# The attention product of a GAT layer as seven matmuls instead of eight, with one buffer fewer and new orders

## The chip, the cores and the metric

The kernel runs on one core of a Trainium2 chip. A core has five engines that work side by side, each through its own queue in order: TensorE (PE, matmuls, with a separate queue PEld for loading weights), VectorE (DVE), ScalarE (ACT), GpSimd (POOL) and SyncE (SP), which here only starts DMAs. Matmul results go to PSUM, 8 banks of 2 KB in each of 128 partitions[...]. The metric is the time of one execution on the device in microseconds. The profile is one further execution, recorded by the hardware profiler.

## What is computed

64 graphs of 256 nodes with 512 features, a 256x256 adjacency for each, all in float32. Two layers, each x = x + layer(relu(layernorm(x)), adjacency).

```python
# layer 0: gated attention, 8 heads of 64
q, k, v = (h @ W.T for W in (Wq, Wk, Wv))
c = softmax(where(adj != 0, q k^T / 8, -inf)) @ v          # per head
gate = sigmoid(concat(c, h) @ Wg.T + bg)
out0 = gate * h + (1 - gate) * c
# layer 1: GAT, one head
Wh = h @ W
e = leaky_relu(Wh a1 [:, None] + Wh a2 [None, :], 0.2)
out1 = elu(softmax(where(adj == 0, -1e9, e)) @ Wh)
```

## The kernel before

A graph's 256 nodes are two tiles of 128 (t = 0, 1), its 512 features two halves of 256 (n = 0, 1). The kernel is written as some 150 named steps for each graph. A table, PLAN, gives each step a time relative to the graph's own start; graph g is shifted by g x ROUND (48), and all steps of all graphs are sorted by that number. This sorted list is the order in which each engine gets its instructions; nothing is reordered later. So about four graphs are in work at once, and after the first few a round repeats for each graph. MOVED holds tables of their own for the first three and the last three graphs, ONCE the order of loading and preparing the weights.

**Products in Strassen's form.** q and k together (qk), v, z (the gate) and wh (Wh) are each a product of a 2x2 block matrix with another. `product` (matmuls on line 369) makes seven block products, named 1 to 7, in three PSUM banks: a takes 1 and then 2, b takes 6, 7 and 4, c takes 5 and 3. Between them partial sums are read out: u1 = a after 1 (copied by ScalarE, line 386), then on VectorE (line 382) u2 = b after 6 + u1, u3 = b after 7 + u1, and the outputs c11 = c after 5 + u3, c10 = b after 4 + u1, c01 = c after 3 + u2; c00 is a after 2, copied by ScalarE. Product 7 adds into the bank that u2 has to have read, 4 into the one that u3 has read, 3 into the one that c11 has read. The sums of the left operand (four for each, steps Sh, Sg, Sc, S1) are GpSimd's (line 353), those of the weights are made once on VectorE (line 308).

**Layer 0.** Step nm0 (ScalarE, line 437) makes the normed tokens h, th turns 32x32 blocks on VectorE (line 445), sh writes them to DRAM in four DMAs (there_h, line 453), fh fetches them transposed (hT, line 460). qk, scores (sc.0 and sc.1, line 566, eight matmuls into four banks each), max on VectorE (line 576), exp on ScalarE (line 586), scale on GpSimd (602) or ScalarE (600), turn, send and fetch to transpose (there_e, eT), we (line 626, banks pc), cT (ScalarE copy, 635), tc (VectorE, into cb), sent and fetched as c. z and the gate: tanh, diff (d<-d,c on GpSimd, 674), plus (x<-x,c on GpSimd, 679), mix (688) and res (x<-d,x, 692) on VectorE. again (ScalarE) makes h once more for the gate.

**Layer 1.** Statistics st1 on VectorE, root1 on GpSimd (rs_l, 427), nb1 on VectorE, nm1 on ScalarE into h1, th1, sh1, fh1 as in layer 0 (there_h and h1T in the profile), wh, ej, lo, lk, gm, gx (the softmax's exponentials), then tg, sg, fg to transpose (there_g, egT). Step po (line 803) multiplies the attention by wh in plain form: for each t four matmuls of 128x128 by 128x256 into one bank, eight for each graph. neg (VectorE, 817: min(po x rec, 0)) and pos (ScalarE, 823: relu(po x rec)) read the bank, xn (827) takes exp of neg, elu (834) and add (GpSimd, 842) finish, and x is stored. For the last two graphs (and the first two in layer 0) transposes go through TensorE instead of DRAM.

**Buffers.** SBUF tiles come from pools by tag: "h" has two buffers and serves h, cb and h1 in turn; "tmp" has five, "e" five, "x" five. A step that writes into a tile waits until the tile that had the buffer before is read for the last time, its DMAs included. In PSUM a tile takes one of eight banks, fixed when the program is built.

The order on TensorE in a steady round before the change: qk.1, z.4 and z.3 of an earlier graph, qk.6, v.1, qk.2, v.6, qk.7, v.5, qk.5, qk.4, po of t=0, qk.3, v.7, v.2, po of t=1, sc.0, we, sc.1, v.3, v.4, and then wh, ej and z of earlier graphs mixed.

Of the kernel before, what the change touches and what calls it, by code (L numbers as in the profile page):

```python
# [23 lines left out]
load@-50.672 st0.0@-48.955 st0.1@-47.821 root0@-38.184 nb0@-37.123 nm0.1@-29.56 nm0.0@-28.012 th.1@-27.761  # L24
th.0@-24.55 edges@-18.194 sh@-17.486 fh@-8.895 qk.1@-5.698 Sh.0@-2.801 Sh.1@-2.517 qk.6@0.316 v.1@0.417
Sh.2@0.475 qk.u1@0.958 qk.2@1.809 v.6@2.371 mask@3.53 qk.u2@3.72 qk.7@4.221 v.5@5.516 qk.5@6.175 qk.u3@7.606
Sh.3@7.626 qk.4@8.199 qk.c11@8.333 qk.c10@9.2 v.u1@9.714 v.u2@9.914 again.1@10.022 qk.3@10.809 qk.c01@10.827
v.7@10.9 v.2@10.953 qk.c00@12.201 sc.0@14.892 max.011@16.85 max.010@18.632 v.u3@21.472 exp.010@22.747
max.000@23.034 v.c11@23.409 max.001@24.188 sc.1@24.213 exp.000@24.365 exp.011@24.661 v.3@24.788 max.110@24.806
max.101@24.817 exp.001@24.929 v.4@26.032 max.100@26.733 rec.00@26.942 exp.101@27.067 v.c01@27.226 exp.110@27.532  # L30
v.c10@27.587 exp.100@29.503 rec.01@31.748 rec.10@32.989 scale.000@33.015 scale.001@34.279 max.111@34.283
turn.000@34.863 exp.111@35.153 scale.011@35.273 turn.001@35.815 scale.101@37.555 rec.11@37.814 turn.101@40.403
v.c00@41.809 scale.010@41.838 scale.100@42.033 send.00@43.292 turn.100@43.322 scale.111@43.998 scale.110@44.728
turn.111@45.825 turn.010@46.602 turn.011@46.632 turn.110@47.102 send.01@49.833 send.10@50.742 Sg.0@50.828
fetch.00@56.979 send.11@57.3 Sg.1@61.926 Sg.3@62.766 fetch.01@63.435 fetch.10@65.008 again.0@66.751 we.01@67.384
fetch.11@67.637 we.00@68.492 we.10@69.53 we.11@70.025 cT.0@70.71 Sg.2@71.512 cT.1@71.604 Sc.0@75.485 z.1@77.916
tc.0@78.544 tc.1@79.25 Sc.1@79.36 z.6@81.96 Sc.2@82.915 z.u1@84.089 z.u2@84.109 sc_c@85.464 z.2@86.278 fc@87.664
z.7@88.275 z.5@89.361 z.u2b@90.783 z.u3@91.761 z.4@92.198 diff.1@93.249 Sc.3@93.522 diff.0@93.841 z.c11@94.163
z.c10@95.683 z.c10b@95.767 z.3@95.773 z.c11b@96.156 plus.1@96.892 tanh.11@98.557 z.c00@98.842 z.c01@99.798
plus.0@99.907 tanh.10@100.162 tanh.00@100.302 mix.1@100.406 res.1@101.571 tanh.01@101.661 mix.0@102.238  # L40
st1.1@102.485 res.0@102.53 st1.0@102.632 root1@102.977 nb1@103.936 nm1.1@103.944 th1.1@103.981 nm1.0@104.039
th1.0@104.288 sh1@113.156 fh1@115.687 S1.0@120.46 S1.1@120.733 wh.1@122.864 wh.6@123.284 wh.u1@123.492
wh.u2@124.276 S1.2@126.087 S1.3@127.493 wh.7@128.378 wh.5@129.278 wh.u3@129.668 wh.c11@129.965 wh.3@130.015
wh.4@130.67 wh.c01@131.832 wh.2@132.003 ej@132.825 wh.c10@133.653 wh.c00@134.025 lo.0@134.129 lo.1@134.703
lk@135.599 gm@135.616 gx.1@140.75 gx.0@141.02 tg@141.763 sg@143.83 gr@152.036 fg@153.077 po.0@153.781
pos.0@153.792 neg.0@153.922 xn.0@156.41 elu.0@157.474 po.1@158.645 add.0@158.767 pos.1@159.243 neg.1@160.27
xn.1@162.323 elu.1@166.01 add.1@166.438 store.1@174.205 store.0@174.205
# [3 lines left out]
load@-167.262 st0.0@-166.518 st0.1@-149.893 nb0@-119.1 nm0.0@-93.712 again.1@-91.245 nm0.1@-79.836  # L51
again.0@-64.37 th.1@-44.14 Sh.0@-41.696 Sh.1@-39.058 Sh.2@-33.746 qk.1@-32.762 edges@-32.058 qk.6@-24.624
qk.u1@-22.066 qk.2@-21.372 qk.u2@-20.805 Sg.0@-17.521 qk.7@-12.436 v.1@-9.392 Sh.3@-8.979 v.6@-8.391
qk.c00@-6.667 qk.u3@-5.057 qk.4@-4.888 Sg.1@-0.322 mask@0.698 qk.5@1.593 qk.c10@3.209 sc.0@5.644 v.u1@9.942
qk.c11@9.945 max.001@10.33 max.011@10.718 Sg.2@13.35 max.000@14.194 qk.3@14.931 exp.001@15.477 qk.c01@15.562
v.u2@15.703 exp.000@15.706 max.010@16.308 sc.1@17.042 max.100@17.52 rec.00@18.128 v.7@18.379 max.101@19.595
exp.100@20.258 max.110@21.168 v.2@21.336 v.u3@21.429 v.5@22.311 scale.001@23.416 max.111@23.712 exp.101@23.777
scale.000@23.974 exp.110@24.415 rec.10@24.965 exp.111@25.826 turn.001@26.665 turn.000@28.936 v.4@29.176
exp.011@29.336 v.c11@29.596 v.c00@30.188 v.3@32.053 rec.11@32.575 scale.101@34.163 v.c10@34.571 exp.010@34.694
turn.101@34.778 rec.01@35.256 scale.110@36.123 scale.100@36.302 scale.011@37.337 turn.100@37.479 send.00@38.912  # L60
send.10@39.674 v.c01@40.035 scale.111@42.42 scale.010@43.268 turn.111@43.418 turn.110@44.351 fetch.00@45.699
turn.010@48.526 Sg.3@48.553 turn.011@48.931 send.11@49.968 send.01@50.543 fetch.10@54.389 fetch.11@60.135
we.00@61.1 we.10@64.692 fetch.01@65.017 we.11@65.565 we.01@66.842 cT.1@67.419 cT.0@68.77 Sc.0@70.118 tc.0@70.581
z.1@70.838 tc.1@73.212 Sc.1@73.23 z.u1@73.542 Sc.2@73.866 z.6@75.497 z.u2@77.891 Sc.3@78.433 z.2@80.627
z.7@81.61 z.5@82.138 z.u2b@83.128 z.u3@85.566 z.4@85.721 z.c11@87.076 z.c00@88.495 sc_c@90.404 tanh.00@91.263
z.3@91.318 z.c10@91.713 fc@93.294 diff.1@94.619 z.c10b@95.258 z.c11b@97.525 tanh.10@98.184 plus.1@98.373
tanh.11@99.383 diff.0@99.752 plus.0@99.825 mix.1@100.146 res.1@101.338 z.c01@102.596 tanh.01@103.055
st1.1@103.531 mix.0@104.285 res.0@104.338 st1.0@104.726 root1@106.188 nb1@107.795 nm1.0@110.078 nm1.1@110.383
th1.0@110.556 th1.1@110.644 sh1@111.628 fh1@113.083 S1.0@119.104 S1.1@120.807 wh.1@121.954 wh.u1@122.591
wh.6@123.635 S1.2@123.913 wh.u2@125.129 S1.3@125.627 wh.5@125.743 wh.7@125.989 wh.2@126.27 wh.u3@126.753  # L70
wh.c11@126.985 wh.4@127.999 wh.3@130.011 wh.c01@131.159 ej@132.88 wh.c10@134.879 lo.1@135.625 wh.c00@135.71
lo.0@137.207 lk@137.282 gm@138.475 gx.1@139.758 gx.0@140.997 gr@141.831 tg@142.453 sg@146.007 fg@149.698
po.1@155.192 po.0@155.734 pos.1@156.08 neg.1@156.318 neg.0@156.913 pos.0@159.131 xn.1@162.457 xn.0@163.013
elu.1@163.216 elu.0@164.233 add.1@164.844 add.0@166.667 store.1@177.808
""",
    1: """
load@-79.223 st0.0@-50.22 st0.1@-47.29 root0@-42.386 nb0@-38.757 edges@-37.434 nm0.0@-33.357 nm0.1@-32.922
th.1@-31.457 qk.1@-22.884 Sh.0@-20.22 Sh.1@-17.198 qk.u1@-17.092 Sh.2@-15.14 qk.6@-15.121 v.1@-13.274 qk.2@-8.08
qk.u2@-4.892 qk.7@-4.473 qk.c00@-3.706 qk.5@-1.564 v.5@0.189 qk.u3@1.902 Sh.3@2.194 v.6@2.96 qk.4@4.184
qk.c11@6.483 v.u1@7.021 qk.c10@7.937 v.u2@8.66 mask@8.958 qk.3@9.075 v.7@10.93 qk.c01@10.959 v.u3@11.262  # L80
sc.0@12.739 max.010@13.434 max.011@16.175 exp.010@16.871 max.001@20.08 max.000@20.575 sc.1@20.654 max.100@21.042
v.4@21.539 v.c11@21.681 max.111@21.684 exp.001@22.615 exp.000@23.152 exp.011@23.363 rec.00@23.965 v.3@23.997
max.101@24.041 exp.111@24.627 max.110@25.446 scale.000@26.187 v.c01@26.675 exp.100@27.482 exp.101@27.764
v.2@28.539 turn.000@29.046 rec.10@29.721 scale.001@31.771 exp.110@32.274 v.c00@32.326 rec.11@33.207
turn.001@33.213 scale.110@33.397 scale.100@33.543 v.c10@35.49 turn.100@36.991 scale.111@37.616 rec.01@37.977
scale.101@38.036 turn.101@39.099 scale.010@39.388 scale.011@39.76 turn.110@40.735 turn.111@44.635
turn.011@47.032 turn.010@47.774 send.00@48.222 send.10@51.087 send.01@52.398 Sg.2@55.238 send.11@56.725
fetch.00@57.149 fetch.10@57.246 fetch.01@58.584 fetch.11@60.705 Sg.0@61.477 we.01@63.116 we.00@64.106
we.10@65.881 Sg.1@66.592 cT.0@66.999 we.11@67.458 cT.1@68.314 Sc.0@68.508 z.1@69.658 tc.1@69.999 again.0@70.426
Sc.1@70.475 tc.0@71.17 z.6@71.96 Sc.2@77.177 sc_c@78.231 Sg.3@79.357 z.u1@79.468 z.2@84.425 z.u2@85.881  # L90
z.7@86.159 z.5@87.606 z.u2b@88.997 z.u3@90.833 Sc.3@92.191 z.c00@93.028 z.4@93.628 z.c11@93.691 fc@95.203
diff.0@95.45 z.c10@96.011 z.c11b@96.41 tanh.00@96.646 z.c10b@96.785 again.1@97.345 tanh.10@97.415 z.3@97.662
plus.1@99.074 tanh.11@99.574 z.c01@100.685 diff.1@100.815 tanh.01@101.285 mix.0@102.146 mix.1@102.203
plus.0@102.369 res.1@103.318 res.0@103.554 st1.1@103.742 st1.0@103.854 root1@104.013 nb1@105.63 nm1.0@106.015
# [819 lines left out]
```

## Time and profile before

| | us |
|---|---|
| median of 3 runs | 3134.52 (3133.42 to 3135.0) |
| the profiled execution, its own time | 3136.5 |
| its span, first to last instruction | 3134.6 |
| TensorE busy in the span | 3104.0 |
| VectorE, GpSimd, ScalarE busy | 2465.1, 1818.2, 1458.2 |
| one steady round (from one graph's qk to the next one's) | 48.07 |

The span is the time on the core; 1.9 us lie around it. Busy times of engines overlap, so their shares don't add up. A group in the profile's list names line, engine, operation and tiles, then count, busy time, mean length in ns, and the idle time ahead of it with what ended it. A matmul in float32 appears as two records. In the views by time a row merges like instructions that follow each other, with start and length.

### The profile page before, as it was taken

Reading aid. Unit: us, or ns where it says so; the run is one execution under the profiler, and the core shown is the slowest. Engines: PE = TensorE matmul, PEld = TensorE weight load, DVE = VectorE, ACT = ScalarE, POOL = GpSimd, SP = SyncE. Lnnn points to the kernel's source line nnn. Section 1 sums busy time; section 2 is a strip of 40 time slices with the busy share of each in tenths; the row PEclk is TensorE's granted clock in tenths of the full one; section 3 lists DMA queues with packets and bytes.
Section 4 is the critical chain, followed back from the end, with each engine's and each line's share of the span. In section 5 each row is a group of like instructions: output and inputs, shape, how many; then the busy total and the mean of one; then the engine's idle time right before and its main releaser. Section 6 shows DMA issues by size and latency. Waiting matters only on the chain.

```text
span 3134.6 us, 61537 instructions
## 1 busy us (share of the span) xinstructions
PE 3104.0 (99%) x19668; PEld 2708.9 (86%) x19668; DVE 2465.1 (79%) x6310; ACT 1458.2 (47%) x4039; POOL 1818.2 (58%) x2502
## 2 busy tenths in 40 slices
PE   9999999999999999999999999999999999999997
PEld 8887888888888888888888888888888888888885
DVE  8887787877877878778778778787787787877875
ACT  4444454454454454544544545445445444454452
POOL 4555565565655655656556556566565565565654
PEclk9999999999999999999999999999999999999998
DMA  7776777777777777777777777777777777777763
GB/s 222 188 196 171 194 197 184 198 188 193 199 188 191 195 186 195 194 189 201 189 185 201 183 196 197 183 200 189 191 201 184 194 198 185 196 189 193 195 160 94
DMA packets 1107154, 593.18 MB, mean 189 GB/s; under 512 B 687632, under 2 KB 1032720, under 8 KB 1106832
## 3 DMA queue, kind: packets, MB, share of 16 engines
q1 hardware_dynamic: 1106832, 589.25, 72.3%
q8 instruction: 158, 2.59, 0.4%
q14 instruction: 164, 1.34, 0.1%
HBM read 306.45 MB, written 282.59 MB: 188 GB/s over the span
## 4 chain that ended last, share of the span: by engine, by line
PE 96%; DVE 2%; DMA 1%; issue 0%; ACT 0%; SPq 0%; POOL 0%; DVEq 0%; ACTq 0%
PE pmb_qk L369 11%; PE pmb_z L369 10%; PE ps L566 8%; PE pc L626 7%; PE pmc_qk L369 7%; PE po L803 7%; PE pma_z L369 7%; PE pma_qk L369 7%; PE pmc_z L369 7%; PE pmb_wh L369 5%; PE pmb_v L369 5%; PE pmc_v L369 4%; PE pmc_wh L369 3%; PE pma_wh L369 3%; PE pma_v L369 3%
## 5 line engine op out<-in xcount | busy, mean ns | idle before, releaser
L586 ACT ACTIVATE e<-e,low 128x256 f32<-128x256 f32 x1024 | 507.9, 501 | 177.8 <-DVE low L576 177.8
L842 POOL TENSOR_TENSOR x<-x,pos 128x512 f32<-128x512 f32 x126 | 160.9, 1278 | 619.0 <-DVE pos L834 619.0
L576 DVE CUSTOM_DVE_ANT_0 e<-ps,mask 128x256 f32<-128x256 f32 x1024 | 375.9, 418 | 40.3 <-PE ps L566 39.2
L437 ACT ACTIVATE h<-x,nb_l,rs_l 128x512 f32<-128x512 f32 x256 | 200.0, 805 | 410.4 <-DMA eT<-there_e 215.0
L602 POOL TENSOR_SCALAR e<-e,rec 128x256 f32<-128x256 f32 x768 | 354.7, 482 | 24.9 <-DVE rec L593 20.7
L608 DVE STREAM_TRANSPOSE eb<-e 128x512 f32<-128x512 f32 x512 | 336.1, 684 | 6.4 <-DMA there_e<-eb 5.7
L566 PE MATMUL ps<-qk 64*128 64x256 f32 x2048 | 257.7, 390 | 0.5 <-ACT neg L827 0.5
L803 PE MATMUL po<-wh,egT 128*128 128x256 f32 x1024 | 245.8, 383 | 4.3 <-DMA egT<-there_g 2.5
L566 PEld LDWEIGHTS ps<-qk 64*128 64x128 f32 x2048 | 192.0, 186 | 60.0 <-DVE low L576 22.9
L817 DVE TENSOR_SCALAR neg<-po,rec 128x512 f32<-128x512 f32 x128 | 95.9, 750 | 183.4 <-ACT pos L823 168.5
L684 ACT ACTIVATE z<-z 128x256 f32<-128x256 f32 x256 | 93.5, 409 | 309.5 <-POOL z L391 190.3
L626 PE MATMUL pc<-eT,v 128*64 128x256 f32 x2048 | 235.6, 382 | 0.0
L427 POOL TENSOR_TENSOR rs_l<-ve_l,mhalf 128x2 f32<-128x2 f32 (+1 forms) x129 | 89.8, 696 | 248.4 <-DVE ve_l L423 232.3
L803 PEld LDWEIGHTS po<-wh,egT 128*128 128x128 f32 x1024 | 192.0, 193 | 30.2 <-DMA egT<-there_g 2.9
L445 DVE STREAM_TRANSPOSE h<-h 128x512 f32<-128x512 f32 x248 | 174.8, 707 | 52.2 <-DMA eT<-there_e 32.6
L626 PEld LDWEIGHTS pc<-eT,v 128*64 128x64 f32 x2048 | 141.1, 137 | 86.3 <-DVE neg L817 18.6
L674 POOL TENSOR_TENSOR d<-d,c 128x512 f32<-128x512 f32 x128 | 164.0, 1282 | 80.1 <-DMA c<-there_c 80.0
L679 POOL TENSOR_TENSOR x<-x,c 128x512 f32<-128x512 f32 x128 | 200.3, 1565 | 0.0
L586 ACT ACTIVATION_READ_ACCUMULATOR e<-e,low 128x1 f32 x1024 | 195.7, 191 | 0.0
L391 POOL TENSOR_TENSOR z<-z,bias 128x256 f32<-128x256 f32 x128 | 90.6, 727 | 168.3 <-DVE z L382 168.2
L416 DVE BATCH_NORM_STATS2 bs_l<-x 128x6 f32<-128x512 f32 x256 | 173.5, 678 | 8.0 <-DMA x<-in_x_dram 5.8
L823 ACT ACTIVATE pos<-po,rec 128x512 f32<-128x512 f32 x128 | 87.9, 687 | 187.2 <-PE po L803 173.9
(152 smaller groups left out, 8141.4 us busy)
## 6 DMA issues: line engine op xcount, KB each, us to landing
there_e<-eb SPq DMA_DIRECT2D x256, 512.0 KB, 3.9
eT<-there_e SPq DMA_DIRECT2D x1024, 128.0 KB, 3.6
there_h<-h SPq DMA_DIRECT2D x496, 128.0 KB, 3.5
there_c<-cb SPq DMA_DIRECT2D x64, 512.0 KB, 2.9
c<-there_c SPq DMA_DIRECT2D x256, 128.0 KB, 3.4
x<-in_x_dram SPq DMA_DIRECT2D x63, 512.0 KB, 5.0
out_dram<-x SPq DMA_DIRECT2D x63, 512.0 KB, 3.1
hT<-there_h SPq DMA_DIRECT2D x248, 128.0 KB, 3.2
```

What stands on the lines that cost most here:

```text
L369: nc.tensor.matmul(s[name, key][(slice(None), *cols)], lhsT, rhs, start=first and i == 0, stop=last and i == len(mms) - 1, skip_group_chec ...
L416: nc.vector.bn_stats(bs, s["x"][:, t, :])
L437: nc.scalar.activation(out, s["x"][:, t, :], AF.Relu, bias=s["nb", layer][:, t:t + 1], scale=s["rs", layer][:, t:t + 1])
L445: nc.vector.transpose(h, h)
L566: nc.tensor.matmul(s["ps", half, jj, i][:, t, :], qk[r:r + DK, 0, jj, t * P:(t + 1) * P], qk[r:r + DK, 1, jj, :], start=True, stop=True,)
L576: nc.vector.tensor_tensor_reduce(e[:, i, t, :], s["ps", half, jj, i][:, t, :], s["mask"][:, t, :], -SCALE, HUGE, ALU.add, ALU.min, accum_o ...
L586: nc.scalar.activation(e, e, AF.Exp, bias=s["low", half][:, jj, i, t:t + 1], scale=-1.0, accum_out=sums[:, jj, i, t:t + 1])
L602: nc.gpsimd.tensor_scalar(e, e, rec, 1.0, ALU.mult, ALU.mult)
L608: nc.vector.transpose(eb[:, :, 4 * i:4 * i + 4, :].rearrange("p b n c -> p n b c"), e)
L626: nc.tensor.matmul(pc[i * DK:(i + 1) * DK, jj, :].rearrange("p (t a c) -> p t a c", t=NT, c=32), s["v"][:, kc, hd * DK:(hd + 1) * DK], s[" ...
L679: nc.gpsimd.tensor_tensor(xt, xt, s["c"][t], ALU.add)
L803: nc.tensor.matmul(po[:, n, :], s["egT"][:, t, kc, :], to_wh(s, g, kc, n)[:, :HH], start=(kc, n) == (0, 0), stop=(kc, n) == (NT - 1, 1), s ...
```

## The change

Step po becomes a `product` too, for all graphs but the last. Its left operand is the transposed attention egT (four 128x128 blocks), its right one the four 128x256 blocks of wh. Each block product is a single matmul (two records). The sums of both operands are GpSimd's, made anew for each graph: Sp.0 to Sp.3 (128x128, into a tile of "tmp") and Rp.0 to Rp.3 (128x256, three in a tile R of a new pool, the fourth in place in wh). The totals u1, u2, u3, c00 to c11 are those of every product; the outputs go to SBUF tiles po of "tmp". neg and pos then read po there, and pos writes in place, so that its own tile is gone. The last graph keeps the old form, as step at.

The pool "h" has one buffer instead of two. h, cb and h1 of the graphs in work now follow each other in that one buffer, each after the sends of the one before have landed.

All tables (PLAN, MOVED, ONCE) are new, so every engine's order changes. The order on TensorE in a steady round is now: qk.1, qk.6, z.3, qk.7, qk.2, qk.5, qk.4, v.6, v.2 (of the graph before), qk.3, po.1, po.6, v.1, po.7, po.5, v.5, po.2, po.4, po.3, sc.0, v.7, we, sc.1, wh.1, v.3, v.4, wh.6, z.1, wh.7, wh.5, z.6, wh.3, wh.2, wh.4, ej, z.5, z.7, z.2, z.4. On VectorE the part that follows u2 of qk is: mix.1, z.c01, res.1, statistics of t=1, mix.0, u3 of qk, res.0, statistics of t=0, c11 of qk, half a turn.100, nb1, c10 of qk, the other half, th1.1, th1.0, a reciprocal, u2 of po, c01 of qk, mask, u3, c11 and c10 of po, nb0, u2 of v, c01 of po, neg.0, max. On ScalarE: tanh, nm1.1, nm1.0, u1 of po, c00 of qk, c00 of v, u1 of v, c00 of po, nm0.1, nm0.0 (of the graph three later), two exp, pos.0, two exp, xn.0, cT.0, again.0, cT.1. On GpSimd: two z biases, scale, diff.1, plus.1, diff.0, plus.0, Sh.3, scale, root1, Sg.0, Rp.1, Sp.0, Sp.1, Sp.2, root0, Sg.1, Sp.3, Rp.3. On SP: there_h of h1 (four), eT (four), h1T (four), there_h of h (four).

The diff, without the tables:

```diff
-        "x": 5, "mask": 3, "hT": 3, "S": 3, "qk": 2, "v": 1, "wh": 1, "e": 5,
-        "cT": 1, "z": 2, "h": 2, "tmp": 5, "U": 3,
+        "x": 5, "mask": 3, "hT": 3, "S": 3, "qk": 2, "v": 1, "wh": 1, "R": 1, "e": 5,
+        "cT": 1, "z": 2, "h": 1, "tmp": 5, "U": 3,
...
+    def left_sum(o, k):
+        return (
+            (o[5], o[8], o[4], ALU.add), (o[6], o[5], o[1], ALU.subtract),
+            (o[7], o[1], o[8], ALU.subtract), (o[3], o[2], o[6], ALU.subtract),
+        )[k]
+
+    def right_sum(o, k):
+        return (
+            (o[7], o[3], o[5], ALU.subtract), (o[6], o[7], o[1], ALU.add),
+            (o[5], o[5], o[1], ALU.subtract), (o[4], o[2], o[6], ALU.subtract),
+        )[k]
...
-    def product(name, shape, todo, dst, biased=False):
+    def product(name, shape, todo, dst, biased=False, until=B):
...
         def multiply(g, n):
+            if g >= until:
+                return
...
-    @step("po.0", "po.1")
+    def left_po(s, g):
+        p, S = s["egT"], lazily(s, "Sp", lambda: new("tmp", [P, 4, P], f"Sp_{g}"))
+        a11, a21, a12, a22 = p[:, 0, 0, :], p[:, 1, 0, :], p[:, 0, 1, :], p[:, 1, 1, :]
+        return {1: a11, 2: a12, 3: S[:, 3, :], 4: a22, 5: S[:, 0, :], 6: S[:, 1, :], 7: S[:, 2, :], 8: a21}
+
+    @step(*each("Sp", 4))
+    def attention_sums(s, g, k):
+        if g < B - 1:
+            nc.gpsimd.tensor_tensor(*left_sum(left_po(s, g), k))
+
+    def right_po(s, g):
+        t = lazily(s, "Rp", lambda: new("R", [P, 3, HH], f"Rp_{g}"))
+        b11, b12, b21, b22 = (s["wh"][:, k, n, :HH] for k in range(NT) for n in range(2))
+        return {1: b11, 2: b21, 3: b22, 4: t[:, 2, :], 5: b12, 6: t[:, 0, :], 7: t[:, 1, :]}
+
+    @step(*each("Rp", 4))
+    def value_sums(s, g, k):
+        if g < B - 1:
+            nc.gpsimd.tensor_tensor(*right_sum(right_po(s, g), k))
+
+    def to_po(s, g, t, n):
+        return lazily(s, ("po", t), lambda: new("tmp", [P, 2, HH], f"po_{g}_{t}"))[:, n, :]
+
+    product("po", [P, HH], lambda s, g, n: [((), left_po(s, g)[n], right_po(s, g)[n])], to_po, until=B - 1)
+
+    @step("at.0", "at.1")
     def attend(s, g, t):
+        if g < B - 1:
+            return
...
     def pos(s, g, t):
-        s["pos", t] = elu_part("pos", g, t)
         po = s["po", t].rearrange("p n f -> p (n f)")
+        s["pos", t] = po if g < B - 1 else elu_part("pos", g, t)
         nc.scalar.activation(s["pos", t], po, AF.Relu, scale=s["rec1"][:, t:t + 1])
```

## The prediction

> **What bounds the kernel now.** I read the page first (busy shares and the chain that ended last), then the busy time in stretches, then the waits of TensorE, then one round of 48.07 us in order of time.
>
> ```profile
> PE 3104.0 (99%) x19668; PEld 2708.9 (86%) x19668; DVE 2465.1 (79%) x6310; ACT 1458.2 (47%) x4039; POOL 1818.2 (58%) x2502
> ...
> PE 96%; DVE 2%; DMA 1%; issue 0%; ACT 0%; SPq 0%; POOL 0%; DVEq 0%; ACTq 0%
> ...
> L803 PE MATMUL po<-wh,egT 128*128 128x256 f32 x1024 | 245.8, 383 | 4.3 <-DMA egT<-there_g 2.5
> ```
>
> The columns of the next view are length, then busy time of PE, PEld, DVE, ACT and POOL with their instruction counts.
>
> ```profile
> 800.00:1200.00 400.00, 400.00 (x2563) 351.44 (x2562) 318.05 (x809) 184.84 (x511) 235.34 (x323) 1.00 0.75 194
> 3050.00:3100.00 50.00, 45.14 (x215) 36.69 (x215) 29.83 (x62) 17.45 (x42) 31.73 (x39) 0.93 0.49 141
> 3100.00:3120.00 20.00, 13.03 (x53) 9.62 (x52) 12.02 (x23) 5.42 (x10) 7.09 (x8) 0.91 0.07 27
> ```
>
> TensorE is busy for all 400 us of the middle stretch, with full clock; of its 30.6 idle us 3.3 lie in the first 60, 6.1 between 260 and 300, where the pipeline fills, and 19.6 after 3060. No other engine comes near: of 48.07 us a round, DVE works 38.2, POOL 28.3, ACT 22.2. So in some 61 steady rounds each matmul taken out is worth its own time, if nothing new makes PE wait.
>
> One round in order of time (start, length, engine, line, operation):
>
> ```profile
> 1536.38 1.90 PE L803 MATMUL po<-wh,egT 128*128 128x256 f32 x8
> 1538.12 1.05 PE L369 MATMUL pmc_qk<-Sh,wq_sb 128*128 128x128 f32 x8
> ```
> ```profile
> 1537.22 2.91 SPq L453 DMA_DIRECT2D there_h<-h  x4
> 1540.24 3.14 SPq L469 DMA_DIRECT2D eT<-there_e  x4
> 1544.29 2.53 SPq L460 DMA_DIRECT2D h1T<-there_h  x4
> ```
> ```profile
> 1527.99 1.72 POOL L679 TENSOR_TENSOR x<-x,c 128x512 f32<-128x512 f32 x1
> ```
> ```profile
> 1528.68 1.57 DVE L692 SCALAR_TENSOR_TENSOR x<-d,x 128x512 f32<-128x512 f32 x1
> ...
> 1531.60 0.66 DVE L692 SCALAR_TENSOR_TENSOR x<-d,x 128x512 f32<-128x512 f32 x1
> ```
>
> Four po matmuls (two records each) move PE on by 1.74 us: 0.435 us a matmul. The normed tokens of layer 1 (h1) need 7.1 us from the first send to the fetch that waits for them. The same DVE operation takes 0.66 us alone and 1.57 while POOL works.
>
> **What the Trainium skill says.** "SBUF — State Buffer", § Who interferes with whom: DVE and GpSimd share one port pair as an exclusive lock; a DVE operation with two SBUF inputs waits until a GpSimd one that reads SBUF is over. The trace agrees: x<-d,x begins 0.69 into POOL's 1.72 us and lasts 0.91 longer than alone. The same section lets tensor_scalar from SBUF enter the two-port mode, which locks too; mask (L496), such an operation, took 0.40 us in one place and 681 ns on average.
>
> **The change, part by part.**
>
> *Matmuls.* 8 become 7 in 63 graphs: 63 x 0.435 = **27.4 us off the path**. Upper bound by the group's row: 245.8/512 = 0.48 each, 30.2. As products of v, wh and z in this same form advance PE by 0.866 per two matmuls, I expect no dearer matmul.
>
> *Added sums.* DVE gets five 128x256 totals at 0.41 (rows of v and z): +2.05 us a graph; neg now reads SBUF, 0.40 for 0.75 twice: -0.7, or nothing if the lock holds it. DVE 39.6 to 40.3 of 47.6 us, 84%. ACT gets two copies, 2 x 0.36; pos moves from PSUM to SBUF, about 0.06 less each: 22.8. POOL gets four 128x256 sums at 0.73 (Rp) and four 128x128 sums (Sp). The trace has no 128x128; from 1.28 for 512 columns and 0.73 for 256 a column costs 2.15 ns, so 0.46: +4.8, POOL 33.1 of 47.6, 70%. None becomes the bound; all lies beside PE as long as each result arrives in time. No DMA is added or removed.
>
> *New waits of PE.* Take qk.1's start as zero and lay the new PE order end to end (qk step 1.79, z 1.73, v or wh 0.87, po 0.435, scores 1.93, we 3.61). po.1 ends at 16.4, po.6 at 16.8, v.1 at 17.7, po.7 follows. po.7 adds into the bank that u2 must have read. PE to DVE takes 0.26 (slot of pmb_wh ends 1506.43, u_wh starts 1506.69), u2 0.42: 0.68 against the 0.87 of v.1, margin 0.2. u1 goes first: 0.20 to ACT, 0.36 copy, then u2 0.42: 0.98 against 1.30. Behind u2 in DVE's queue stand qk.c01, mask, u3, c11; they give po.4 and po.3 some 0.7. po.6 needs Sp.0 and Sp.1 on POOL; added up from rs1 (12.7) over Sg.0 and Rp.1 they end at 15.1, margin 1.3. The wait is nothing when DVE stands ready, at most 0.7 when a lock holds the transposes ahead. I take 0.05.
>
> *u3 of qk.* In the new DVE order mix.1, z.c01, res.1, one statistics and mix.0 come ahead of it. Two are held by POOL's d and x additions. Worked through: end 10.4, qk.4 wants it at 10.7.
>
> *One h buffer.* nm0 of graph g+3 on ACT now waits until all four there_h1 DMAs of graph g have landed. Ahead: z.3 ends at 5.3; DVE z.c01, res, statistics, rs1 on POOL, nb1, two nm1 (0.71 each), two transposes end at about 16.2 (17.6 in the round shown). In ten rounds that I looked at, the fetch that needs all four started 5.7 to 5.8 us after the first send in five, 6.6 to 7.1 in five. So nm0 starts at 22.0 or 22.9. Queued behind it on ACT: two relus 1.42, four exponentials with read-outs 1.96, pos.0 0.55, xn.0 0.54, cT.0 0.57: cT.0 is out at 27.0 or 27.9; then again.0 and cT.1 at 28.2 or 29.1. Who waits: the last score bank of sc.1 (its bank held pc that cT.0 reads) at 28.1, and wh.1 (bank of cT.1) at 29.07. Margin 1.0 in good rounds, about nothing in the others, where 0.1 to 0.2 of hand-over makes PE wait. The trace of before has no such wait, its two buffers hide it; bounds: 0 (landings always early) and 1.4 a round (transposes as late as before, landing 7.1). A gain is excluded: a removed buffer frees nobody. I take 0.05. hT, h1T and eT keep 1 us or more in this addition; cb's turn in the buffer (sent at 26, wanted at 33.7) has the same.
>
> *Orders at the ends.* The last two Strassen po (61, 62) stand in a stretch where PE already waits (2.50 us for egT at 3067.8, 1.06 and 0.23 for h after it, 2.85 for h at 3106). Their u1, u2, Sp chain is two handovers longer, 0 to +4; I take +1. The head moves a few products around, and the 6.1 us where the pipeline fills may shrink or grow: -3 to +3, taken 0.
>
> **Sum** against the profiled execution: 3136.5 (span 3134.6 and 1.9 around it) - 27.4 + 61 x 0.1 + 1 = 3116.2. The median of the runs lies 2.0 under the profiled one, so **3114**.
>
> **Rivals.**
> *A, full gain:* every margin holds: 3134.5 - 27.4 = 3107, ends -3 to +4. For it: PE never waited for these engines before, at 79% DVE. Chance 0.25.
> *B, the forecast:* waits of 0.03 to 0.33 a round, 3109 to 3128. Chance 0.33.
> *C, waits eat it:* 0.33 to 0.53 a round, within 0.2% (6.3 us, about what a measurement of this kernel tells from no change). Chance 0.10.
> *D, slower:* the single h buffer sets the round. Place: ACT's nm0, behind the landing of there_h1, and PE at sc.1 and wh.1. It decides once the mean wait passes 0.435 a round: transposes of h1 ending at about 16.9 rather than 16.2 do that, for then the late half of the landings costs some 0.9. With 0.9 a round, 61 x 0.9 - 27.4 + 1 = +28.5, 3163; with 0.65, 3148. For it: mix and res are both behind POOL's locks, POOL has 17% more to do, and DVE has 2 us less to catch up. Chance 0.32.
> *E, it does not do what it says:* the new order shows seven one-matmul products per graph; excluded but for the last graph, which keeps the old form.
>
> **Numbers.** Faster 0.25 + 0.33 = 0.58, same 0.10, slower 0.32. The range 3105 to 3150 leaves out the best ends of A and half of D. The likeliest side alone, A with B: 3105 to 3128.
>
> **What would show it.** PE records of po fall from 1024 to about 900 and PE's busy time by some 27 us; a round takes 47.6 to 47.8 us between two equal products. If PE shows idle at po.7 <- DVE u2, the margin of 0.2 failed; at qk.4 <- DVE u3, the locks; at ps or wh.1 <- ACT cT, the h buffer, and ACT's h<-x would then wait for a there_h landing. D is right, and I am wrong, if the round is over 48.07 us. Idle at PE for Sp or Rp would mean that POOL's added 4.8 us do not fit.

## Result and the profile after

The changed kernel takes 3206.8 us (median of 4 runs, 3204.91 to 3207.68) against 3134.76 for the kernel before on the same chip: a ratio of 1.023, 95% interval 1.0212 to 1.0248. It is slower by 72 us where 21 us less were forecast, and lies outside the range. The profiled execution took 3206.9, its span 3205.1.

The page of the changed kernel, busy shares, then the chain that ended last:

```profile
PE 3160.6 (99%) x19542; PEld 2672.1 (83%) x19542; DVE 2599.1 (81%) x6625; ACT 1490.4 (46%) x4165; POOL 2208.9 (69%) x3006
...
PE 86%; POOL 7%; issue 3%; DVE 1%; DMA 1%; SPq 0%; ACT 0%; POOLq 0%; DVEq 0%; ACTq 0%
```

126 matmul records are gone, as they should be (19668 to 19542), and still PE is "busy" for 57 us more. So the busy share of matmuls does not show that PE waits. The chain does: PE's part of it falls from 96% to 86%, and GpSimd (POOL) has 7%, where it had none. The Trainium skill warns of the busy share: "Perfetto Trace Analysis", § Identifying the Most-Contended Engine, says that the busy share of matmuls is not a good measure of how close a kernel is to its roofline, since matmuls are pipelined, and names the matmul work done as a share of the peak and the busy share of weight loads instead. The trace agrees: with matmuls at 99% in both, PEld falls from 86% to 83%. Of this fall 1.2 points are loads that are gone (2708.9 to 2672.1 us), the rest is the longer span. In the middle stretch (columns as before: length, then PE, PEld, DVE, ACT, POOL; at the end the granted clock, the busy share of the DMA engines, GB/s):

```profile
800.00:1200.00 400.00, 398.06 (x2461) 336.96 (x2460) 327.11 (x837) 188.79 (x533) 281.97 (x388) 1.00 0.73 189
```

The length of a round tells it most directly. I take it from the ej matmuls (pe<-ident,wh) of one graph to those of the next, over the 48 rounds from graph 9 to graph 57: 48.07 us before, 49.29 after, each round the same within 0.4. 48 x 1.23 = 59 of the 70.5 us by which the span grew; the start gives 6 and the end 5.5.

Where in the round? The po part is as laid out. PE of the changed kernel in order of time:

```profile
1518.72 0.60 PE L390 MATMUL pma_po<-wh,egT 128*128 128x256 f32 x2
...
1520.45 0.63 PE L390 MATMUL pmb_po<-Rp,Sp 128*128 128x256 f32 x2
...
1523.61 2.00 PE L589 MATMUL ps<-qk 64*128 64x256 f32 x16
...
1526.59 3.91 PE L649 MATMUL pc<-eT,v 128*64 128x256 f32 x32
1530.44 1.56 PE L589 MATMUL ps<-qk 64*128 64x256 f32 x8
1532.16 1.13 PE L589 MATMUL ps<-qk 64*128 64x256 f32 x8 [0.16 <-DVE low L599]
1533.23 1.14 PE L390 MATMUL pma_wh<-w_sb,h1T 128*128 128x257 f32 x4
...
1536.15 1.14 PE L390 MATMUL pmb_wh<-w_t,S 128*128 128x257 f32 x4
```

qk.1 of this round starts at 1502.77. po.1 comes at +15.95, po.7 (the second row) at +17.68, sc.0 at +20.84: within 0.1 of the sum of the steps. Then it slips. The two halves of sc.1 start 1.72 apart (1530.44, 1532.16) where eight such records take 0.97 (half of the 1.93 of all sixteen). The row shows only 0.16 of idle; the rest hides in the modelled end of the row ahead. The wait named is low, the output of the row maxima. VectorE at that time:

```profile
1524.67 0.49 DVE L867 TENSOR_SCALAR neg<-po,rec 128x512 f32<-128x512 f32 x1
1527.73 0.42 DVE L599 CUSTOM_DVE_ANT_0 e<-ps,mask 128x256 f32<-128x256 f32 x1 [2.57 <-DMA h1T<-there_h]
```

In the kernel before, sc.0 and the first maximum:

```profile
1543.45 2.00 PE L566 MATMUL ps<-qk 64*128 64x256 f32 x16
1545.50 0.43 DVE L576 CUSTOM_DVE_ANT_0 e<-ps,mask 128x256 f32<-128x256 f32 x1 [0.39 <-PE ps L566]
```

The first maximum starts 4.12 us after sc.0 (1523.61); in the kernel before it was 2.05. VectorE stood idle for 2.57 us ahead of it, with the scores long there. The DMA named brings nothing that a maximum reads; the waits by line (total us, times, longest) name another candidate nearly as often:

```profile
DVE e L599 <- DMA h1T<-there_h: 77.0, 30, 2.6
DVE e L599 <- PE pc L649: 72.8, 28, 3.1
...
PEld pmb_wh L390 <- POOL S L375: 27.3, 58, 0.8
...
ACT h L460 <- DMA there_h<-h: 21.5, 20, 2.7
```

The addresses in the built program name the cause. The first maximum writes its masked scores into a tile of the pool "e". In the changed kernel that tile (e of half 0, pair 0) got the buffer of eT of half 0, pair 0 of the graph before, which is last read by the first products of we, and those begin at 1526.59. In the kernel before, the corresponding tile got the buffer of an eb of the graph before, sent a round earlier. So PE's we holds the buffer, the maxima start after it, they free the last score bank at 1532.1, and PE's sc.1 wants that bank. GpSimd's sums S for wh come late too: they stand in its queue behind the scaling of e, which follows the maxima and the exponentials. ACT's wait for a landing of there_h, the sign that the prediction had named for the h buffer, is there too, but small (21.5 us in the whole run).

### The profile page after: what moved, and what is told of

Same layout as the page of the kernel before. It is cut to its first block, busy times and chain, and to the rows that moved or that the text cites. A ratio compares the mean times of both kernels' runs of the same rounds, so it can differ in the third digit from the quotient of the medians.

```text
span 3205.1 us, 62526 instructions
## 1 busy us (share of the span) xinstructions
PE 3160.6 (99%) x19542; PEld 2672.1 (83%) x19542; DVE 2599.1 (81%) x6625; ACT 1490.4 (46%) x4165; POOL 2208.9 (69%) x3006
## 4 chain that ended last, share of the span: by engine, by line
PE 86%; POOL 7%; issue 3%; DVE 1%; DMA 1%; SPq 0%; ACT 0%; POOLq 0%; DVEq 0%; ACTq 0%
PE pmb_qk L390 10%; PE pmb_z L390 10%; PE pc L649 7%; PE pma_qk L390 7%; PE pmc_qk L390 7%; PE pma_z L390 7%; PE pmc_z L390 7%; PE ps L589 6%; PE pmb_wh L390 6%; POOL S L375 5%; PE pmb_v L390 4%; PE pmc_wh L390 3%; PE pma_v L390 3%; PE pmb_po L390 3%; PE pmc_v L390 2%
## 5 line engine op out<-in xcount | busy, mean ns | idle before, releaser
L625 POOL TENSOR_SCALAR e<-e,rec 128x256 f32<-128x256 f32 x768 | 396.1, 530 | 679.3 <-PE ps L589 632.4
L631 DVE STREAM_TRANSPOSE eb<-e 128x512 f32<-128x512 f32 x512 | 348.6, 691 | 6.9
L589 PE MATMUL ps<-qk 64*128 64x256 f32 x2048 | 297.4, 395 | 9.9 <-DVE low L599 9.5
L649 PE MATMUL pc<-eT,v 128*64 128x256 f32 x2048 | 249.9, 386 | 5.4 <-DMA eT<-there_e 4.4
L892 POOL TENSOR_TENSOR x<-x,po 128x512 f32<-128x512 f32 x126 | 185.3, 1472 | 10.7 <-DVE po L884 10.7
L409 ACT COPY u_qk<-pma_qk 128x512 f32<-128x512 f32 x64 | 37.5, 586 | 298.5 <-PE pma_qk L390 298.4
L468 DVE STREAM_TRANSPOSE h<-h 128x512 f32<-128x512 f32 x248 | 165.3, 684 | 0.3 <-ACT h L460 0.3
L405 DVE TENSOR_TENSOR u_po<-pmb_po,u_po 128x256 f32<-128x256 f32 x126 | 52.7, 419 | 113.3 <-ACT u_po L409 102.6
L390 PE MATMUL pmb_wh<-w_t,S 128*128 128x257 f32 x512 | 138.4, 392 | 4.6 <-DVE u_wh L405 0.6
L390 PE MATMUL pma_qk<-hT,wq_sb 128*128 128x128 f32 x1024 | 136.1, 276 | 2.7 <-DVE hT L501 2.7
```

The lines of the kernel that those rows point to most:

```text
L390: nc.tensor.matmul(s[name, key][(slice(None), *cols)], lhsT, rhs, start=first and i == 0, stop=last and i == len(mms) - 1, skip_group_chec ...
L589: nc.tensor.matmul(s["ps", half, jj, i][:, t, :], qk[r:r + DK, 0, jj, t * P:(t + 1) * P], qk[r:r + DK, 1, jj, :], start=True, stop=True,)
L625: nc.gpsimd.tensor_scalar(e, e, rec, 1.0, ALU.mult, ALU.mult)
L631: nc.vector.transpose(eb[:, :, 4 * i:4 * i + 4, :].rearrange("p b n c -> p n b c"), e)
L649: nc.tensor.matmul(pc[i * DK:(i + 1) * DK, jj, :].rearrange("p (t a c) -> p t a c", t=NT, c=32), s["v"][:, kc, hd * DK:(hd + 1) * DK], s[" ...
L892: nc.gpsimd.tensor_tensor(xt, xt, s["pos", t], ALU.add)
```

## The experiments

**Theory 1:** the first maxima wait for the e buffer. **Theory 2:** the single h buffer sets the round (rival D of the prediction). **Theory 3:** the added sums hold up GpSimd or VectorE. Another buffer of 4 KB for h does not fit beside the new pool R, so the runs with two h buffers use one gate weight for both halves of z; their expectations say so.

### One buffer for the first maxima

```diff
-"e": 5,
+"e": 4, "f": 1,
-e = lazily(s, ("e", half, jj), lambda: new("e", ...
+e = lazily(s, ("e", half, jj), lambda: new("e" if half or jj else "f", ...
-eb = lazily(s, ("eb", half, jj), lambda: new("e", ...
+eb = lazily(s, ("eb", half, jj), lambda: new("f" if half > jj else "e", ...
```

> The changed kernel with the five e buffers split into four and one: e of half 0, pair 0 (the tile of the first two row maxima) and eb of half 1, pair 0 (the block-turned copy that is sent last) take turns in the one. All orders, the single h buffer and the Strassen form stay. Theory 1 (the row maxima wait for a buffer that the products with eT of the graph before still read, and the second half of the scores waits for the maxima): the 2.57 us of idle ahead of the first maximum fall below 0.7, the 0.75 us lost inside sc.1 and the late sums S are gone, a round goes from 49.27 to between 47.6 and 48.1, the time from 3207 to 3106 to 3135. Theory 2 (the single h buffer) and theory 3 (the added sums on GpSimd and VectorE come late): the time stays between 3195 and 3212.

Measured: 3183.6 us, ratio 1.0163 (1.0146 to 1.018). A gain of 21 us by the ratios: theory 1 wanted 3106 to 3135, the other two 3195 to 3212, so neither number came. The banks of PSUM are no rival here: in the built program they follow one another as in the changed kernel in all graphs but two, and the shortest rounds are 47.85. The rounds are no longer equal: 47.85 to 49.92, mean 48.54. What stands in the long ones is theory 2's wait. By line, then one such round on VectorE, SP, ScalarE and PE:

```profile
ACT h L460 <- DMA there_h<-h: 110.7, 35, 4.6
```
```profile
1556.75 0.69 DVE L631 STREAM_TRANSPOSE eb<-e 128x512 f32<-128x512 f32 x1
1557.38 1.26 DVE L468 STREAM_TRANSPOSE h<-h 128x512 f32<-128x512 f32 x2
```
```profile
1557.51 1.73 SPq L492 DMA_DIRECT2D eT<-there_e  x4
...
1559.81 4.20 SPq L476 DMA_DIRECT2D there_h<-h  x4
```
```profile
1568.47 1.52 ACT L460 ACTIVATE h<-x,nb_l,rs_l 128x512 f32<-128x512 f32 x2 [4.52 <-DMA there_h<-h]
...
1573.00 0.56 ACT L658 COPY cT<-pc 128x512 f32<-128x512 f32 x1
```
```profile
1571.30 1.56 PE L589 MATMUL ps<-qk 64*128 64x256 f32 x10
1573.62 1.13 PE L589 MATMUL ps<-qk 64*128 64x256 f32 x6 [0.76 <-ACT cT L658]
```

h1's first send is issued at 1559.81, the last one has landed when nm0 starts at 1568.47, 8.66 us later. Behind nm0 in ScalarE's queue stand the exponentials and cT.0, and PE's last score bank waits for cT.0: place and chain are those of rival D. The wait of nm0 grew from 21.5 to 110.7 us when the e wait went.

But this edit has a hand in it. The transposes of h1 end at 1558.64, and its first send leaves 1.2 us later, behind four fetches of eT and a send in SP's queue. In this built program the eT of half 0, pair 1 got the buffer of e of half 1, pair 0 of the same graph, so its fetch waits for the last transpose of that tile (1556.75). In the 40 rounds from graph 12 on, it starts 14.06 us after qk.1 (median), against 11.12 in the changed kernel; the sends of h1 start at +16.37 against +15.22, their last landing is at +23.3 against +21.2, and nm0 starts at +23.55 against +21.31. The split took one wait away and brought another.

### Two h buffers, and both

```diff
-"cT": 1, "z": 2, "h": 1,
+"cT": 1, "z": 2, "h": 2,
```

> The changed kernel with two h buffers again. To make room, the cell products use the hidden-side weights for the context as well, so its output is not the reference's, and the loading and the sums of one weight at the start are left out (0 to 10 us of the head). Theory 2 (the single h buffer sets the round): a round of 47.6 to 48.1 us, 3100 to 3135. Theory 1 (the e buffer) and theory 3 (added sums): a round of 49.0 to 49.3, 3185 to 3207.

Measured: 3204.76 us, ratio 1.0229 (1.0214 to 1.0245); every round 49.27. The single h buffer alone explains nothing of the time of the changed kernel.

> Both at once: the split e buffers of the first run and the two h buffers of the second (with the same weights in place of the context's, and the same load and sums left out). Theory 1: as the first run, 47.6 to 48.1 us a round, within 10 us of it. Theory 2: as the second run. Theory 3 (the added sums): a round of 49.0 or more, 3185 or more. If each buffer carries a part, this run is faster than both of them by more than 10 us.

Measured: 3144.17 us, ratio 1.0035 (1.0023 to 1.0046); rounds of 47.85. This is faster than both single edits by over 10 us, the last case of its expectation. Mean round (us):

| | one h buffer | two |
|---|---|---|
| first maximum behind we (pool of 5) | 49.29 | 49.27 |
| own buffer (4 + 1) | 48.54 | 47.86 |

The gains do not add up: two h buffers gain 0.02 with the e wait in place and 0.68 without it. The 0.68 is not the single h buffer's price alone. In the run with both, the pool e has yet another succession, the fetch of that eT starts at +11.27 and the sends of h1 at +15.21, so the late sends of the first experiment are gone as well. How much of the 0.68 is the single buffer, and how much the late sends, was not separated. The right column is the cleaner comparison: with two h buffers in both, the e wait costs 1.42 us a round. (In these two runs banks of sc.1 change hands as well; the shortest rounds of the first experiment reach 47.85 without that.) PE and VectorE with both, in the order of time:

```profile
1543.02 2.00 PE L591 MATMUL ps<-qk 64*128 64x256 f32 x16
1546.01 3.67 PE L651 MATMUL pc<-eT,v 128*64 128x256 f32 x32
1549.61 2.00 PE L591 MATMUL ps<-qk 64*128 64x256 f32 x16
1551.54 1.13 PE L392 MATMUL pma_wh<-w_sb,h1T 128*128 128x257 f32 x4
...
1554.24 1.03 PE L392 MATMUL pmb_wh<-w_t,S 128*128 128x257 f32 x4
```
```profile
1544.58 0.43 DVE L601 CUSTOM_DVE_ANT_0 e<-ps,mask 128x256 f32<-128x256 f32 x1
```

The maximum starts 1.56 us after sc.0, and sc.1 runs through, all 16 records in one row. Against the changed kernel's round, start by start, PE is equal up to we; then 0.24 are gained from we to sc.1 (3.60 for 3.85), 0.86 from sc.1 to wh.1 (1.93 for 2.79), and 0.33 around wh.6, which no longer waits for S. That is the whole 1.43 between these rounds.

### The stalls at the ends

The run with both was still 11 us over the kernel before, at rounds 0.21 shorter: the split pool loses, as I reckoned it, some 8 us at the start and 7.5 near the end. I put these stalls down to graphs 0 and 61 and gave one more eb of each to the single buffer.

```diff
-"f" if half > jj else "e"
+"f" if (half, jj) in one_buffer(g) else "e"
+def one_buffer(g):
+    return [(1, 0)] + {0: [(0, 1)], B - 3: [(1, 1)]}.get(g, [])
```

> The first run's split buffers, with the first and the third-last graph giving one more of their eb tiles to the single buffer (the first run had stalled in both, some 8 us at the start and 7.5 us at the end). One h buffer. Both theories (the e buffer and the h buffer each cost something in the steady rounds) want the first run less the two stalls: 3184 - 15 = 3169, between 3160 and 3176, with rounds that still change between 47.85 and 49.9 us. If the stalls belong to something else, it stays at 3180 or more.

Measured: 3183.26 us, ratio 1.0153 (1.0138 to 1.0168): nothing gained.

> The run with both buffers (split e, two h; the hidden-side weights used for the context too, one weight's load and sums left out), with the two stalls at the ends mended in the same way: 3144 - 15 = 3129, between 3120 and 3136, steady rounds 47.85. Together with the run of the late norm it tells what the single h buffer costs if ScalarE does not wait for it: equal within 6 us if nothing.

Measured: 3143.62 us, ratio 1.0029 (1.0017 to 1.004): nothing gained here either. I had taken the wrong graphs. The third turn of graph 1 and that of graph 62 stalled; in the built program eb of half 0, pair 1 has the buffer of the eb ahead there, whose send had still to land. VectorE of the run of 3183.26 us, the third turn of graph 1, then that of graph 62:

```profile
75.43 0.71 DVE L634 STREAM_TRANSPOSE eb<-e 128x512 f32<-128x512 f32 x1 [9.26 <-DMA there_e<-eb]
...
3043.70 0.71 DVE L634 STREAM_TRANSPOSE eb<-e 128x512 f32<-128x512 f32 x1 [6.43 <-DMA there_e<-eb]
```

### The norm moved back on ScalarE

nm0.1 and nm0.0 behind cT.1, th.1 and th.0 behind the second neg, around the first maximum of half 1, and sh behind them, in the steady graphs:

```diff
-nm0.1@-29.303 nm0.0@-26.84 th.1@-26.684 th.0@-25.569 sh@-25.308
+nm0.1@-24.340 nm0.0@-24.338 th.1@-23.680 th.0@-23.660 sh@-22.900
```

> As the run beside it (split e buffers, ends mended, one h buffer), and in the steady rounds the norm of the next tokens (nm0 on ScalarE) stands behind cT.1, with its transposes and its send behind that. If the single h buffer costs time because nm0 waits at the head of ScalarE's queue for the landing of h1, with exponentials and copies of scores behind it: no wait of nm0, every steady round 47.8 to 47.9, as with two buffers, and 3120 to 3135. If it costs time through the buffer's own chain (norm, transpose, send, then cb, then h1), rounds stay over 48.3, 3155 or more.

Measured: 3302.11 us, ratio 1.0533 (1.0517 to 1.0549), mean round 50.64. The second case holds, more strongly than I had put it. From its waits by line:

```profile
DVE cb L671 <- DMA there_h<-h: 96.2, 58, 3.2
...
PE pmc_wh L390 <- DVE wh L405: 62.0, 57, 2.0
```

nm0 now hardly waits for a landing (6.5 us in all), but h is sent later (1531.76, that is +31.97, against +26.39 with two buffers) and cb, which takes the same buffer next, waits for it in 58 rounds. Behind cb in VectorE's queue stand totals of wh that free a bank, and PE waits for those. The single buffer leaves a gap: nm0 not before h1 has landed, h sent early enough for cb.

> The changed kernel with the late norm alone: five e buffers in one pool as in the change. If the two waits hide one another, the row maxima still wait for the buffer that the products with eT read: rounds of 49.1 to 49.3, 3198 to 3210. If the h wait were the cause and the e wait its effect: rounds below 48.5, 3165 or less.

Measured: 3333.08 us, ratio 1.0632 (1.0616 to 1.0648), mean round 51.61, outside both cases: the later norm costs 2.3 us a round on top of the e wait, so this run says nothing on whether the two waits hide one another.

### Both mended, and a version faster than both kernels

eb of half 0, pair 1 takes turns in the single buffer too, in all graphs but 61; nm0 stands between cT.0 and cT.1, th behind rec.00 and v.c11. The first pair of lines is set against the run of 3183.26 us, the second against the changed kernel.

```diff
-    return [(1, 0)] + {0: [(0, 1)], B - 3: [(1, 1)]}.get(g, [])
+    return {B - 3: [(1, 0), (1, 1)], B - 2: [(0, 1)]}.get(g, [(1, 0), (0, 1)])
-nm0.1@-29.303 nm0.0@-26.84 th.1@-26.684 th.0@-25.569 sh@-25.308 ... again.0@71.536
+nm0.1@-25.360 nm0.0@-25.358 th.1@-25.140 th.0@-25.050 sh@-25.000 ... again.0@71.700
```

> Split e buffers (in the one: e of half 0 pair 0, then eb of half 0 pair 1, then eb of half 1 pair 0, with other turns in the last graphs), one h buffer, the whole computation. In the steady rounds the norm of the next tokens stands between cT.0 and cT.1 on ScalarE, its transposes behind rec.00 and v.c11 on VectorE; a run before had put both some 2 us later, behind cT.1 and the second neg, and so had delayed cb, which takes the same buffer. If the single h buffer costs only by where its users stand: rounds 47.8 to 48.1 and the two end stalls gone, 3120 to 3140. If its chain (h1 sent, norm, transposes, h sent, cb) does not fit in a round: nm0 or cb still wait, rounds of 48.4 or more, 3160 or more.

Measured: 3130.7 us (21 runs), ratio 0.9988 (0.9982 to 0.9995), mean round 47.98, end stalls gone. The whole computation in some 3.5 us less than the kernel before, 0.1%: the interval leaves out a ratio of 1, but the gain is small. cb still waits in 34 rounds, 22.7 us in all. Two things changed here: the place of the norm, and the succession in the pool e, by which the fetch of the eT of half 0, pair 1 starts at +11.46 again rather than +14.06. So how much of the gain in the steady rounds is the norm's was not separated.

> The same turns in the single e buffer, two h buffers, the change's orders (the hidden-side weights used for the context too, one weight's load and sums left out). The stalls at the two ends came from eb of half 0, pair 1 waiting for the landing of the eb before it; it has another buffer now: 3144 - 15 = 3129, between 3118 and 3136, rounds 47.85. If the stalls stay, 3140 or more.

Measured: 3122.99 us, ratio 0.9964 (0.9951 to 0.9978), every round 47.85. So one h buffer with the new place of nm0 costs 0.13 us a round, 6 to 8 us in all, against two with the norm in the change's own place (this run also does without the load of one weight). Mending the ends gave 21 us where 15 had been reckoned, 12 of them up to graph 9 and 6 behind graph 57. The middle stretch of this run, to set beside that of the changed kernel:

```profile
800.00:1200.00 400.00, 400.00 (x2554) 346.55 (x2554) 337.56 (x861) 195.25 (x537) 284.26 (x391) 1.00 0.75 193
```

PE loads weights for 346.6 us of 400 rather than 337.0, with VectorE and GpSimd busier than in the changed kernel: their load was not the limit there.

### The same wait in the old kernel

The kernel before, with the tile of its first maximum and the first eT in one buffer of their own:

```diff
-"e": 5,
+"e": 5, "f": 1,
-e = lazily(..., lambda: new("e", ...
+e = lazily(..., lambda: new("f" if jj > half and 4 < g < 58 else "e", ...
-eT = new("e", ...
+eT = new("f" if not half and not jj and 4 < g < 58 else "e", ...
```

> The kernel before with its old orders and plain po, in which the tile of the first row maxima and the first eT share one buffer of their own in the steady graphs (the pool of five stays for the rest; hidden-side weights for the context, as in the others with little room). So the first maximum must wait for the first products with eT, as in the changed kernel, with one buffer more than before in all. Theory 1: the first maximum starts 1.1 us later (1546.6 in the round shown), and a round goes from 48.07 to between 48.3 and 49.2: 3150 to 3200. If the wait alone costs nothing (the maxima have slack, and the loss in the changed kernel has another cause): 48.07, 3125 to 3138.

Measured: 3198.16 us, ratio 1.0206 (1.0192 to 1.022), mean round 49.29, the same as the changed kernel's and just over the 48.3 to 49.2 of theory 1. VectorE and PE:

```profile
1577.15 0.42 DVE L577 CUSTOM_DVE_ANT_0 e<-ps,mask 128x256 f32<-128x256 f32 x1 [2.27 <-PE pc L627]
```
```profile
1573.23 2.00 PE L567 MATMUL ps<-qk 64*128 64x256 f32 x16
1575.15 1.95 PE L627 MATMUL pc<-eT,v 128*64 128x256 f32 x16
1578.18 1.95 PE L627 MATMUL pc<-eT,v 128*64 128x256 f32 x16 [1.08 <-ACT cT L636]
```

The first maximum starts 3.92 us after sc.0 rather than 2.05, so 1.87 later where 1.1 had been expected. Old orders, plain po, two h buffers, one e buffer more than before, and 1.2 us a round are lost: such a wait can turn up, and cost as much, without any part of the change. PE pays at another place, though: the whole loss lies between the starts of we and sc.1. The built program of this run gives the second bank of we the bank of the first, so PE waits for cT.0 within we; that the banks fell so because score banks come free later is likely but not shown. How much of the 1.2 is the late maximum and how much this choice of bank was not separated, so the price of the wait rests on the 1.42 above, not on this run.

### Without the added sums

```diff
-if g < B - 1:
+if g < B - 1 and not 4 < g < 58:
     nc.gpsimd.tensor_tensor(*left_sum(left_po(s, g), k))
```

(likewise for the four of Rp, with left_po and right_po giving blocks of the attention and of wh in place of the sums)

> The run with two h buffers and split e, with the eight GpSimd sums of po (Sp, Rp) left out in graphs 5 to 57; the products then multiply blocks of the attention and of the values themselves, so the output is not the reference's. Theory 3 (the added sums load GpSimd or hold VectorE's port, and cost the round something): below 47.7 us a round. If they are hidden beside TensorE, as predicted: 47.8 to 47.9, within 4 us of the run with the sums.

Measured: 3122.55 us, ratio 0.9964 (0.995 to 0.9977), every round 47.81. GpSimd works 242.4 of the middle 400 us rather than 284.3, some 5 us a round less, and the round is 0.04 us shorter. Theory 3 falls as far as GpSimd's sums go; the five totals on VectorE and the two copies on ScalarE stay in, in this run and in all rounds of 47.85.

## Why the prediction was wrong, point by point

- **Matmuls.** The records fell by 126, and the products of po advance PE by 0.43 to 0.44 each (0.48 once). Right. Of 0.435 us a round 0.22 arrive when both buffers are free (48.07 to 47.85). In the round shown of the run with both, hand-overs cost 0.05 at po.7, 0.09 ahead of sc.0, 0.19 behind v.7 and 0.10 at wh.1 beyond the laid-out steps: 0.43, where the round before had 0.17. The short single products ahead of sc.0 leave less cover; that is read from the trace, not tested.
- **Added sums.** Right: Sp took 0.46 as estimated, VectorE 81% and GpSimd 69% (84% and 70% of a shorter round forecast), and the run without GpSimd's sums shows that they cost 0.04 us a round. The expected waits did not come: po.7 loses 0.05, in the whole run po waits 3.2 us for Sp and 1.1 for u2, qk.4 nothing.

```profile
L390 PE MATMUL pmb_po<-Rp,Sp 128*128 128x256 f32 x252 | 79.1, 396 | 4.3 <-POOL Sp L829 3.2 <-DVE u_po L405 1.1
```

- **The step that failed** is the list of new waits of PE, which holds none for a buffer of e. The half sentence "hT, h1T and eT keep 1 us or more in this addition" asks when eT arrives, not how long we holds its buffer and who gets it next. I looked for waits where the diff shows new operands or a smaller pool. The e pool keeps its five buffers, so I priced it at nothing. But new orders change which tile follows which in a pool. In the term 61 x 0.1 of the sum, 0.1 should have been 1.66 (49.29 against 48.07 - 0.435 = 47.63): 1.42 from the e buffer, 0.02 from the h buffer, 0.22 from the hand-overs. With 1.66 the sum gives 3209, against 3206.8 measured.
- **One h buffer.** In the changed kernel the 0.05 held: a second h buffer gives back 0.02. D needed transposes of h1 that end at about +16.9 rather than +16.2. They end at +15.2 in the changed kernel, the last landing is at +21.2 (20.7 to 21.7 in 40 rounds), and nm0 starts at +21.31, against +21.04 with two buffers and the 22.0 or 22.9 of the prediction; so D's margin of 1.0 is kept. In the first experiment place and chain were those of D, but there SP's queue held the sends back. The 0.68 found between one buffer and two lies in D's 0.65 to 0.9 partly by luck, as the late sends are in it. What a single h buffer costs once the e wait is gone and the sends leave in time was not measured.
- **The ends.** Forecast +1 in all, measured in the run of 3123 us -7 up to graph 9, of which 1 to 2 are the shorter rounds (the kernel before has one round of 55.42 there, this run none over 50.5), and +4.7 behind graph 57.
- **Forecast B.** With both waits away the change does nearly what B said: 3123 to 3131 where 3109 to 3128 stood. The sign of the change hung on who follows whom in a few buffers, the tile of the first maxima above all.
- **Left open:** why the built program gives the first maximum the buffer of an eT while that of an eb is free by then (its tile is sent at 1516.81, and the third of the e tiles gets it). The order of all instructions decides it in some way; no run was made to see how. What a single h buffer costs in the old orders has no number: with one, their steps wait for each other in a circle (a deadlock).

## What to carry to other kernels

When orders are rewritten, list for every pool which tile takes over whose buffer and who reads the old one last; a pool whose size does not change can still gain a wait, and the load of the engines says nothing of it. An edit that takes a wait away does the same again: look in its own program and trace for the wait that it brings. Gains of single edits need not add up, so take each wait away alone and both together before one is acquitted. Read a PE that waits in the length of a round, in the distance between starts and in the loading of weights, not in its busy time.

## What was not expected of the hardware

In the first experiment the four DMAs of h1 took 6.4 to 8.5 us from the first send to the last landing (median 6.9, rounds between 600 and 2600 us), in the kernel before 5.5 to 6.9 (median 5.7), at nearly the same DMA share in the middle stretch (0.74 and 0.75). The sending makes the difference: the fourth send left 3.6 us after the first (median) rather than 2.1. What slows it was not tested. And eight more GpSimd sums a round, some 5 us of its work, cost only 0.04 us of a round with VectorE at 83%.
